# The convolution tail on half tiles: two row pairs of four streams, 64x32 products, and a copy of the odd pairs

## The chip, the cores and the metric

The kernel runs on one core of one Trainium2 chip. A core has a matrix engine (PE, with a separate row PEld for loading its stationary operand), a vector engine (DVE), a scalar engine (ACT), a general engine (POOL) and a queue that issues transfers (SP). PE reads SBUF and writes PSUM, which has eight banks of 512 fp32 columns per partition; DVE and ACT carry results out of PSUM ("eviction"). The metric is the device time of one launch in microseconds. A profile is one further execution, recorded by the hardware.

## The reference, cut to what matters

The input is four images of 16 channels and 512 x 512 pixels, in fp32. Layer 0 (a depthwise convolution, window attention and a perceptron) comes first and is not touched, except for where its result is stored. Then follow:

```
# layer 1: quantise to 8 bits by the largest magnitude, 3x3 convolution, normalise over the whole batch
step = max(abs(x)) / 127;  xq = clip(round(x / step), -127, 127) * step
y = conv3x3(xq, wq);  y = (y - mean(y)) * gamma / sqrt(var(y) + 1e-5) + beta
z = clip(y, 0, 6)
# layer 2: two 3x3 convolutions and a residual
h = relu(conv3x3(z, w1) + b1);  x = conv3x3(h, w2) + b2 + z
# layer 3: a 3x3 convolution and a perceptron 16 -> 128 -> 16 for every pixel
y = conv3x3(x, conv_w);  out = x + w2' relu(w1' y + b1') + b2'
```

Mean and variance of layer 1 need its convolution over the whole batch before any z can be made, so this convolution is done twice: once for the statistics, once for the result.

## The kernel before, in words

`window_attention` is layer 0. It stores its result block by block (`_store_block`, line 88) into `x1`, a buffer in DRAM. `conv_layers` (line 938) is all the rest, called the tail here.

**Tiles.** The image is cut into S = 4 strips of 128 rows. A tile (an index `mm` of M = 64) holds one row pair of each strip of each image: 128 partitions are 4 images x 2 rows x 16 channels, and the free dimension is 4 strips x 512 columns. Row pairs of z, x and the quantised q are offset by one row against those of h and y, so that a 3x3 convolution of an output pair needs two neighbouring input pairs ("sides"), each with three column shifts (dx). Offsetting each layer by one row keeps this alternation.

**A convolution** is therefore 2 sides x 3 shifts x 4 images x 4 strips = 96 products. `_conv_turn` (927) issues four of them: image i's 32 partitions are the contraction, strip j chooses the 32 output partitions, so that all sixteen 32x32 positions of PE's array are used. Layer 1 multiplies in bf16 (integers, exact), the others in fp32; an fp32 product appears in the trace as two matmul instructions. Each shows with its own weight load.

**Turning.** After a convolution, image i's result lies in bank i with the strips along the partitions, so each convolution swaps the two roles. z, h, x, y alternate between the layouts; the residual x is needed in the other layout at the end, and `turned` (1129) copies it with 16 transfers per tile into `xi`.

**The statistics stage** (1037 to 1047): per tile, POOL scales for quantising and ACT rounds (`scaled`, `rounded`), PE convolves into one of two sets of four banks, and DVE takes `bn_stats` of each bank. The loads run eight tiles ahead, in buffers that the main loop uses later. Then `bn_aggr` and a few small operations give scale and shift.

**The main loop** (1210 to 1235) runs 73 steps of 28 slots. In step t, PE convolves y for tile t-4, x for t-3, h for t-1 and z for t; the perceptron's tile is t-6. The table CONVS gives 20 slots of a step to the convolutions. In the other eight, `hidden` (1149) makes the perceptron's 128 hidden values of one row pair by four 32x32 products and one eviction with relu, five of eight by ACT and three by DVE. The four images run two slots apart (LAG), so that products of four row groups, of convolutions and perceptron, are mixed all the time. Convolutions have banks 0 to 3, hidden values banks 4 to 7. At a step's end `outputs` (1165) multiplies the 32 hidden tiles by 128x32 weights, adds the residual and stores the tile.

**Order.** Within the tail the program's order is kept as it is written on PE, DVE, ACT and SP (`manual_schedule`, line 992); waits are set where operands need them. An instruction that waits holds back all behind it on its engine or queue. Evictions of a convolution are `done0` to `done3` (for z, h, x, y), with `clipped` for z; the quantising of tile t+2 is spread over slots 10 to 21.

Of the kernel before, what the change touches and what calls it, by code (L numbers as in the profile page):

```python
# [29 lines left out]
S = 4  # L30
M = H // S // 2
# [19 lines left out]
    ("l3_b1", 1), ("l3_b2", 1), ("head", 2), ("par", 2), ("edge", 2),  # L51
# [36 lines left out]
def _store_block(nc, x1, src, b, r0, cols, queues=None):  # L88

    n = WS // 2  # L90
    s, m = divmod(r0 // 2, M)
    parts = [(1, m, s, 0, n), (0, m + 1, s, 0, n)]
    if m + n == M and s < S - 1:
        parts[1:] = [(0, m + 1, s, 0, n - 1), (0, 0, s + 1, n - 1, 1)]
    for r, mm, ss, at, k in parts:
        part = 32 * b + C * r
        (next(queues) if queues else nc.sync).dma_start(
            x1[mm : mm + k, part : part + C, ss, cols].rearrange("m c x -> c m x"),
            src.rearrange("c (m r) x -> c m r x", r=2)[:, at : at + k, 1 - r],
        )  # L100
# [14 lines left out]
def conv_chain(ctx: ExitStack, tc: tile.TileContext, x, xw, mats, vecs, cqs, cws, hots, out):  # L115
# [6 lines left out]
    x1 = dram.tile([M + 1, P, S, W], F32, name="x1")  # L122
    with tc.tile_pool(name="zeros", bufs=1) as one:
        zero = one.tile([C, W], F32, name="zero")
        nc.vector.memset(zero, 0.0)
        for b in range(B):
            at = 32 * b
            nc.sync.dma_start(x1[0, at : at + C, 0], zero)
            nc.sync.dma_start(x1[M, at + C : at + 2 * C, S - 1], zero)
# [776 lines left out]
def _load_pairs(nc, t, x1, mm):  # L906


    if mm < 0:
        nc.vector.memset(t[:, 0], 0.0)  # L910
        nc.sync.dma_start(t[:, 1:S], x1[M + mm, :, 0 : S - 1])
    elif mm < M:
        nc.sync.dma_start(t, x1[mm])
    else:
        nc.sync.dma_start(t[:, 0 : S - 1], x1[mm - M, :, 1:S])
        if mm == M:
            nc.sync.dma_start(t[:, S - 1], x1[M, :, S - 1])
        else:
            nc.vector.memset(t[:, S - 1], 0.0)


def _turns():

    return [(side, dx, i) for side in range(2) for dx in range(3) for i in range(4)]


def _conv_turn(nc, p, weights, src, side, dx, i):

    for j in range(4):
        nc.tensor.matmul(  # L930
            p[i][_quad(j)], weights[_quad(i), side, dx, :],
            src[side][_quad(i), j, dx : dx + W],
            start=side == 0 and dx == 0, stop=side == 1 and dx == 2,
        )
# [3 lines left out]
def conv_layers(ctx: ExitStack, tc, x1, out, cw, cq, sw, m, v, peak):  # L938
# [5 lines left out]

    nc = tc.nc
    ld = ctx.enter_context(tc.tile_pool(name="l3l", bufs=2))
# [4 lines left out]
    conv_banks, hid_banks = banks[0:4], banks[4:8]  # L963
# [3 lines left out]
    def ring(name, n, dt=F32):  # L967
        tiles = rings[name] = [
            act.tile([P, 4, WP], dt, name=f"{name}{i}") for i in range(n)
        ]  # L970
        return lambda mm: tiles[mm % n]
# [5 lines left out]
    qs = ring("q", 3, BF16)  # L977
    zs, hs, xs, xi, ys = ring("z", 3), ring("h", 2), ring("x", 2), ring("xi", 3), ring("y", 3)
    for name in "qz":
        border(name)  # L980

    edge_b1 = act.tile([P, 2], F32, name="edge_b1")
# [3 lines left out]

    stats = rings["h"][0].rearrange("p s x -> p (s x)")[:, 0 : M * B * 6].rearrange(
        "p (r s) -> p r s", s=6
    )
# [13 lines left out]
    def outside(mm):  # L1003

        return 0 if mm < 0 else S - 1 if mm >= M else None

    loaded = {}

    def load(mm, t=None):
        if t is None:  # L1010
            t = ld.tile([P, S, W], F32, tag="x", name=f"tx{mm}")
        loaded[mm] = t
        _load_pairs(nc, loaded[mm], x1, mm)

    def scaled(mm, at=slice(0, S), engine=nc.vector):
        t = loaded[mm][:, at]
        engine.tensor_scalar(t, t, ix, ROUND, ALU.mult, ALU.add)  # L1017

    def rounded(mm, at=slice(0, S)):
        nc.scalar.activation(  # L1020
            inner(qs(mm))[:, at], loaded[mm][:, at], AF.Identity, bias=unround
        )

    flat = [
        t.rearrange("p s x -> p (s x)")[:, 0 : S * W].rearrange("p (s x) -> p s x", x=W)
        for t in rings["y"] + rings["xi"] + rings["x"]
    ]
    AHEAD = len(flat)  # L1030
    for mm in range(AHEAD):
        load(mm, flat[mm])
    sx, ix = quant_step(nc, act, act, peak, "x")
    for mm in range(2):
        scaled(mm)
        rounded(mm)
    for mm in range(M):
        if mm + 2 <= M:
            scaled(mm + 2, engine=nc.gpsimd)
            rounded(mm + 2)  # L1040
        p = banks[4 * (mm % 2) : 4 * (mm % 2) + 4]
        for turn in _turns():
            _conv_turn(nc, p, cq, (qs(mm), qs(mm + 1)), *turn)
        for b in range(B):
            nc.vector.bn_stats(stats[:, mm * B + b, :], p[b])  # L1045
        if mm + AHEAD <= M:
            load(mm + AHEAD, flat[mm % AHEAD])
    for name in ("x", "xi", "y"):
        border(name)
    for mm in (-2, -1):  # L1050
        load(mm)
        scaled(mm)
        rounded(mm)
    load(0)

# [14 lines left out]
    border("h")  # L1072
# [15 lines left out]
    shift = act.tile([P, 1], F32, name="shift")  # L1088
    ms = mul(mean, scale, "ms")
    nc.vector.tensor_tensor(shift, v("beta"), ms, ALU.subtract)  # L1090


    def done0(mm, b):
        z, p = inner(zs(mm)), conv_banks[b]
        if b % 2:
            nc.vector.tensor_scalar(z[:, b], p, scale, shift, ALU.mult, ALU.add)  # L1096
        else:
            nc.scalar.activation(z[:, b], p, AF.Identity, bias=shift, scale=scale)

    def clipped(mm, b):  # L1100
        z = inner(zs(mm))
        nc.vector.tensor_scalar(z[:, b], z[:, b], ACT_MAX, 0.0, ALU.min, ALU.max)
        if outside(mm) is not None:
            nc.vector.memset(z[_quad(outside(mm)), b], 0.0)

    def done1(mm, s):
        h, p = inner(hs(mm)), conv_banks[s]
        if (s, mm) in ((0, -1), (S - 1, M + 1)):
            nc.vector.memset(h[:, s, :], 0.0)
        elif (s, mm) in ((0, 0), (S - 1, M)):  # L1110
            e = 0 if mm == 0 else 1
            nc.scalar.activation(
                h[:, s, :], p, AF.Relu, bias=edge_b1[:, e : e + 1],
                scale=v("edge")[:, e : e + 1],
            )
        elif s % 2:
            nc.vector.tensor_scalar(h[:, s, :], p, v("l2_b1"), 0.0, ALU.add, ALU.max)  # L1117
        else:
            nc.scalar.activation(h[:, s, :], p, AF.Relu, bias=v("l2_b1"))

    def done2(mm, b):
        x, z = inner(xs(mm)), inner(zs(mm))
        nc.vector.scalar_tensor_tensor(
            x[:, b, :], conv_banks[b], v("l2_b2"), z[:, b, :], ALU.add, ALU.add
        )
        if outside(mm) is not None:
            nc.vector.memset(x[_quad(outside(mm)), b], 0.0)

    def turned(mm):

        if outside(mm) is None:
# [45 lines left out]

    SLOTS, LAG = 28, 2
    CONVS = {}
# [183 lines left out]
```

## Time and profile before

| | us |
|---|---|
| median of 3 runs (6274.52 to 6279.33) | 6274.99 |
| the profiled execution, device time | 6290.58 |
| its span, first to last instruction | 6288.8 |
| PE busy | 6035.0 (96%) |
| ACT busy | 4051.9 (64%) |
| DVE busy | 3220.5 (51%) |
| statistics stage | about 3472 to 3737 |
| main loop, filling | about 3745 to 3924 |
| main loop, steady and end | about 3924 to 6289 |

Busy time of PE counts products whose ends are modelled and that overlap in several positions of the array, so it tells that PE had work, not that it ran at its best. A group of instructions is named by its line, engine and operation, the tiles that it writes and reads, and the shape: 32*32 stands for active rows times columns of the array. The weight loads (PEld) overlap the products. The chain that ended last holds PE for 23% of the span by line 930, 11% by line 1154 and 7% by line 1170.

### The profile page before, as it was taken

How to read it: one execution, taken by the hardware profiler on the slowest of the kernel's cores; microseconds unless marked ns; L12 is line 12 of the kernel's file. 1: busy time of each engine (PE TensorE's matmuls, PEld its weight loads, DVE VectorE, ACT ScalarE, POOL GpSimd, SP SyncE). 2: the span in 40 equal slices, each digit the busy share in tenths (PEclk: the TensorE clock that was granted, in tenths of full speed). 3: DMA queues.
4: the chain of work that ended last, by engine and by line, in shares of the span. 5: the costliest groups of instructions: out<-in, count | busy, mean ns of one | idle time of the engine just before them, and what ended most of it. 6: DMA issues, size and time to landing. Idle time of an engine off the chain costs nothing. (4 is left out here: it accounts for less than half of the span.)

```text
span 6288.8 us, 316830 instructions
## 1 busy us (share of the span) xinstructions
PE 6035.0 (96%) x146976; PEld 3792.6 (60%) x146976; DVE 3220.5 (51%) x4719; ACT 4051.9 (64%) x5602; POOL 150.7 (2%) x127
## 2 busy tenths in 40 slices
PE   8999999999999999999999459999999999999999
PEld 4666666666666666666665336566555555655565
DVE  3444444444444444444444564555555555555555
ACT  4777777777777777777777443555555455555454
POOL 0000000000000000000000530000000000000000
PEclk9999999999999999999999778999999999999999
DMA  3233333232323232323332751222222222222221
GB/s 82 59 76 60 77 60 77 59 78 59 78 59 78 59 78 59 78 58 69 68 61 38 288 201 57 89 86 87 87 89 84 86 89 87 90 86 84 84 82 55
DMA packets 567525, 515.29 MB, mean 82 GB/s; under 512 B 349008, under 2 KB 478352, under 8 KB 545712
## 3 DMA queue, kind: packets, MB, share of 16 engines
q1 hardware_dynamic: 564688, 493.47, 30.0%
q8 instruction: 1154, 18.91, 1.3%
q0 software_dynamic: 1216, 1.05, 0.1%
q14 instruction: 179, 1.47, 0.1%
q10 hardware_dynamic: 288, 0.39, 0.0%
HBM read 225.87 MB, written 134.48 MB: 57 GB/s over the span
## 5 line engine op out<-in xcount | busy, mean ns | idle before, releaser
L1154 PE MATMUL tb<-y,mat 32*32 32x512 f32 x16384 | 1861.5, 597 | 25.0 <-issue 25.0
L1160 ACT ACTIVATE hid<-tb,vec 128x512 f32<-128x512 f32 x1280 | 871.6, 688 | 1143.0 <-PE tb L1154 1082.0
L369 ACT ACTIVATE e<-pair 128x1024 f32<-128x1024 f32 x1024 | 992.4, 1021 | 394.5 <-PE pair L361 394.5
L297 PE MATMUL pair<-x,taps 32*32 32x512 f32 x18432 | 926.5, 604 | 2.6 <-ACT y L308 1.3
L930 PE MATMUL tb<-z,cw 32*32 32x512 f32 x12864 | 902.8, 608 | 5.3 <-issue 5.2
L930 PE MATMUL tb<-h,cw 32*32 32x512 f32 x12672 | 905.8, 604 | 0.0
L1162 DVE TENSOR_SCALAR hid<-tb,vec 128x512 f32<-128x512 f32 x768 | 576.0, 750 | 616.2 <-PE tb L1154 330.0
L930 PE MATMUL tb<-x,cw 32*32 32x512 f32 x12480 | 852.2, 598 | 0.0
L930 PE MATMUL tb<-q,cq 32*32 32x512 bf16 x12672 | 680.8, 447 | 133.7 <-issue 68.8
L417 PE MATMUL bank<-y,fc_e 32*32 32x512 f32 x8192 | 683.1, 603 | 0.9 <-DVE y L409 0.9
L361 PE MATMUL pair<-g,y 32*128 32x128 f32 x16384 | 654.3, 285 | 25.9 <-ACT y L308 24.3
L1154 PEld LDWEIGHTS tb<-y,mat 32*32 32x32 f32 x16384 | 531.1, 103 | 242.7 <-issue 140.1
L361 PEld LDWEIGHTS pair<-g,y 32*128 32x128 f32 x16384 | 544.3, 187 | 214.7 <-issue 109.5
L297 PEld LDWEIGHTS pair<-x,taps 32*32 32x32 f32 x18432 | 602.4, 103 | 97.0 <-issue 17.5
L422 ACT ACTIVATE hid<-bank,f1b 128x512 f32<-128x512 f32 x1024 | 644.8, 685 | 15.5 <-PE bank L417 7.5
L353 DVE COPY yt<-bank 128x512 f32<-128x512 f32 x512 | 347.3, 688 | 550.4 <-PE bank L348 530.8
L930 PEld LDWEIGHTS tb<-h,cw 32*32 32x32 f32 x12672 | 507.3, 104 | 186.8 <-issue 27.0
L380 PE MATMUL bank<-e,yt 128*32 128x128 f32 x16384 | 556.6, 276 | 2.6 <-issue 1.6
L396 DVE TENSOR_TENSOR o<-bank,r 128x512 f32<-128x512 f32 x512 | 354.0, 691 | 372.7 <-ACT r L395 356.8
L385 PE MATMUL bank<-e,hot 128*32 128x512 f32 x4096 | 535.8, 593 | 0.0
L930 PEld LDWEIGHTS <-cq 32*32 32x32 bf16 x12672 | 320.1, 92 | 347.4 <-issue 265.7
L380 PEld LDWEIGHTS bank<-e,yt 128*32 128x32 f32 x16384 | 418.1, 110 | 110.6 <-DVE yt L353 52.8
(163 smaller groups left out, 6770.4 us busy)
## 6 DMA issues: line engine op xcount, KB each, us to landing
x<-in_xw_dram SPq DMA_DIRECT2D x32, 2600.0 KB, 10.8
y<-y SPq DMA_DIRECT2D x2048, 32.0 KB, 2.2
tx<-x SPq DMA_DIRECT2D x64, 1024.0 KB, 5.5
xi<-x SPq DMA_DIRECT2D x1024, 64.0 KB, 2.5
out_dram<-xi SPq DMA_DIRECT2D x64, 1024.0 KB, 4.9
x<-xo SPq DMA_DIRECT2D x1974, 32.0 KB, 1.7
y<-x SPq DMA_DIRECT2D x24, 1024.0 KB, 6.1
xi<-x SPq DMA_DIRECT2D x24, 1024.0 KB, 5.2
```

The lines of the kernel that those rows point to most:

```text
L297: nc.tensor.matmul(bank(u)[quad(vv)], taps[quad(u), tap, :], xts[n // 2][quad(u), vv, dy : dy + WS, at : at + BW], start=tap == 0, stop=ta ...
L361: nc.tensor.matmul(bank(u)[:, P * jj : P * jj + P], y2[quad(u), vv, jl + jj].rearrange("p w t -> p (w t)"), g[quad(u), vv, jl + jj].rearra ...
L369: nc.scalar.activation(e[:, 2 * i : 2 * i + 2].rearrange("p u j t -> p u (j t)"), pairs[i], AF.Exp,)
L380: nc.tensor.matmul(b[quad(u), P * jj : P * jj + P], yt[:, jj, quad(u)], e[:, u, jj, :], start=True, stop=True,)
L385: nc.tensor.matmul(d[quad(u)], own, e[:, u].rearrange("p j t -> p (j t)"), start=True, stop=True,)
L396: nc.vector.tensor_tensor(o[:, vv, jl : jl + 4].rearrange("p j h t -> p (j h t)"), b, r, ALU.mult)
L417: nc.tensor.matmul(b[quad(k)], fc1[quad(vv), quad(k)], y[quad(vv), u, :], start=True, stop=True,)
L422: nc.scalar.activation(hd, b, AF.Gelu, bias=f1b)
L930: nc.tensor.matmul(p[i][_quad(j)], weights[_quad(i), side, dx, :], src[side][_quad(i), j, dx : dx + W], start=side == 0 and dx == 0, stop= ...
L1154: nc.tensor.matmul(p[_quad(c)], w1[_quad(b), 1 - par, 32 * c : 32 * c + 32], inner(ys(mm + par))[_quad(b), s, :], start=True, stop=True,)
L1160: nc.scalar.activation(hd, p, AF.Relu, bias=v("l3_b1"))
L1162: nc.vector.tensor_scalar(hd, p, v("l3_b1"), 0.0, ALU.add, ALU.max)
```

## The change

The tail is written anew on tiles of half the size, and `x1` and the output take a layout to match.

A tile now belongs to one of two pairs of images and one of TP = 64 positions. S is 2: the image has two halves of 256 rows. The 128 partitions are 2 halves x 2 neighbouring row pairs x 2 rows x 16 channels; the free dimension is the 2 images x 512 columns. The four (pair, image) combinations are the streams of a half.

A convolution contracts over 64 partitions, both sides at once, so that three shifts are left: 3 shifts x 2 pairs x 2 images x 2 halves = 24 products of 64 rows and 32 columns (`convolve`). An output pair that straddles two tiles needs its two input pairs in one block of 64 partitions. A second copy of each tile, shifted by one pair, serves these (qo, zo, ho, xo beside qe, ze, he, xe). `shift` makes it by four transfers on SP for each of q, z, h and x: 32 partitions x 2 images x 514 columns each. The result of a convolution has the row pairs and images along the partitions and the halves in the two banks. Weights come in a second copy with the sides exchanged.

The perceptron makes its hidden values in waves: four products of 32 rows and 128 columns, from the four quarters of y into four banks, then four evictions. 16 such products a tile, in two stretches of eight. The output products are 128x32 as before, 16 a tile.

All eight banks are taken in turn by all stages (`take`). In a step, the stages stand one after another: y, eight wave products, x, h, quantising of tile T+2, eight wave products, z, outputs. There are N + 6 = 140 steps, as N = 2 x 67.

The statistics stage uses 64x64 products: both pairs of one image at once, with zero blocks in the weights (`cq2`); 24 products a half tile, bf16. Its loads run 18 half tiles ahead. A load is two transfers of 256 KB. A clip of z is one operation of 1024 columns where there were four of 512; scaling and rounding in the main loop likewise have 1024 columns.

The diff, cut to its core:

```diff
-S = 4
-M = H // S // 2
+S = 2
+TP = H // S // 4
-    x1 = dram.tile([M + 1, P, S, W], F32, name="x1")
+    x1 = dram.tile([H // 2 + 1, 2 * C, B, W], F32, name="x1")
 ...
+def _load_pairs(nc, t, x1, g, tt):
+    for r in range(S):
+        m = r * H // 4 + 2 * tt
+        k = min(2, H // 2 + 1 - m)
 ...
+        nc.sync.dma_start(
+            t[64 * r : 64 * r + 32 * k],
+            x1[m : m + k, :, 2 * g : 2 * g + 2].rearrange("m c f x -> (m c) f x"),
         )
 ...
-    conv_banks, hid_banks = banks[0:4], banks[4:8]
+    turn = itertools.count()
+    def take(n):
+        return [banks[next(turn) % 8] for _ in range(n)]
 ...
+    qe, qo = ring("qe", 3, BF16), ring("qo", 3, BF16)
+    ze, zo, he, ho = ring("ze", 4), ring("zo", 3), ring("he", 2), ring("ho", 2)
+    xe, xo, ye = ring("xe", 5), ring("xo", 3), ring("ye", 3)
 ...
+    for n in range(LAST):
+        if n + 2 < LAST:
+            scaled(n + 2, nc.gpsimd)
+            rounded(n + 2)
+        if n % (TP + 1) < TP:
+            p = take(S)
+            for k in range(2):
+                for dx in range(3):
+                    for f in range(2):
+                        for r in range(S):
+                            nc.tensor.matmul(
+                                p[r][_half(f)], cq2[_half(r), k, dx, :],
+                                qe(n + k)[_half(r), f, dx : dx + W],
+                                start=k == 0 and dx == 0, stop=k == 1 and dx == 2,
+                            )
+            for r in range(S):
+                nc.vector.bn_stats(stats[:, done, :], p[r])
+                done += 1
+        load_flat(n + AHEAD)
 ...
+    def shift(n, e, o):
+        for i in (1, 3):
+            nc.sync.dma_start(o(n)[_quad(i)], e(n)[_quad(i)])
+        if n % K:
+            for i in (0, 2):
+                nc.sync.dma_start(o(n - 1)[_quad(i)], e(n)[_quad(i)])
+    def quantised(n):
+        scaled(n)
+        rounded(n)
+        shift(n, qe, qo)
 ...
+    def convolve(weights, pair):
+        p = take(2)
+        for dx in range(3):
+            for w in range(2):
 ...
+                src, odd = pair[w]
+                for f in range(2):
+                    for r in range(2):
+                        nc.tensor.matmul(
+                            p[r][_quad(2 * f + w)], weights[_half(r), odd, dx, :],
+                            src[_half(r), f, dx : dx + W],
+                            start=dx == 0, stop=dx == 2,
+                        )
+        return p
 ...
+    def stage_z(n):
 ...
+        p, z = convolve(cq, ((qe(n), 0), (qo(n), 1))), inner(ze(n))
+        nc.scalar.activation(z[:, 0], p[0], AF.Identity, bias=shift_by, scale=scale)
+        nc.vector.tensor_scalar(z[:, 1], p[1], scale, shift_by, ALU.mult, ALU.add)
+        nc.vector.tensor_scalar(z, z, ACT_MAX, 0.0, ALU.min, ALU.max)
+        outside(ze(n), t)
+        shift(n, ze, zo)
 ...
+        for q in range(4):
+            w, f = divmod((k + q) % 4, 2)
+            par = w ^ (q % 2)
+            src = ye(n + (w and not q % 2))
             nc.tensor.matmul(
+                p[q], w1[_quad(q), 1 - par, :], inner(src)[_quad(q), f, :],
+                start=True, stop=True,
+            )
+        for q in range(4):
+            w, f = divmod((k + q) % 4, 2)
+            hd = ld.tile([P, W], F32, tag="hid", name=f"hid{n}_{k}_{q}", bufs=24)
+            if next(count) % 8 in (0, 2, 3, 5, 6):
+                nc.scalar.activation(hd, p[q], AF.Relu, bias=v("l3_b1"))
+            else:
+                nc.vector.tensor_scalar(hd, p[q], v("l3_b1"), 0.0, ALU.add, ALU.max)
 ...
+    for T in range(N + 6):
+        if T + 3 < N:
+            load(T + 3, *item(T + 3, -1, TP + 1))
+        stage_y(T - 4)
+        units = wave(T - 6, 0) + wave(T - 6, 1)
+        stage_x(T - 3)
+        stage_h(T - 1)
+        if T + 2 < N:
+            quantised(T + 2)
+        units += wave(T - 6, 2) + wave(T - 6, 3)
+        stage_z(T)
+        outputs(T - 6, units)
```

`stage_h` evicts one bank by ACT and one by DVE, `stage_x` both by DVE with the residual from ze, `stage_y` one each; `stage_h` and `stage_x` end with a `shift`. `outputs` adds the residual in xe and stores the tile. At an image's edge, rows outside are set to zero, and h's edge rows get a scale of zero from a third column of `edge`.

## The prediction

> **What bounds the kernel now.** I read the shares by slice of the span first, then the stretches, then the chain in order of time, then the matrix unit's timeline for one period. In the stretches (first figure the length, then PE, weight loads, DVE, ACT, POOL, with busy time and instructions; last the granted clock, the DMA share, GB/s):
>
> ```profile
> 0.00:3400.00 3400.00, 3332.89 (x74953) 2164.21 (x74956) 1574.37 (x2148) 2628.15 (x3536) 4.67 (x8) 1.00 0.32 67
> ...
> 3472.00:3737.00 265.00, 142.85 (x6144) 98.87 (x6144) 165.32 (x268) 131.77 (x67) 125.84 (x79) 0.74 0.70 266
> 3745.00:3924.00 179.00, 175.54 (x3960) 108.19 (x3964) 82.22 (x159) 61.92 (x93) 0.00 (x0) 0.82 0.21 67
> ...
> 4038.00:6188.00 2150.00, 2123.33 (x56512) 1287.01 (x56496) 1253.55 (x1939) 1091.50 (x1703) 0.00 (x0) 1.00 0.28 85
> ```
>
> The first 3461 us are attention; the change touches only its store addresses. The tail is a statistics stage (3472 to 3737), a filling stage on a lowered clock (3745 to 3924) and a steady loop in which PE never rests, DVE is 58% and ACT 51% busy. The chain in order of time (start, length, group) gives the period and the cost of the output products:
>
> ```profile
> 4038.69 7.06 PE tb L1170 x64
> 4050.07 0.87 PE tb L930 x15
> 4053.93 1.07 PE tb L930 x31
> 4076.15 7.06 PE tb L1170 x64
> ```
>
> From 3923.6 to 6249.4 there are 62 periods: 37.5 us per old tile. Of these, 7.06 are the 64 output products (128x32), 16 groups of four, 441 ns each; 30.4 are the 928 products of 32x32. Those are slower than streaming: 832 fp32 in 52 groups of sixteen and 96 bf16 in 6 should take 52 x 428 + 6 x 220 = 23.6 us, with 428 ns the distance of consecutive passes inside L1170 in the single records. The timeline says where 7 us go (PE only; start, length, line, count):
>
> ```profile
> 4050.35 0.74 PE L1154 MATMUL tb<-y,mat 32*32 32x512 f32 x4
> ...
> 4050.80 0.72 PE L1154 MATMUL tb<-y,mat 32*32 32x512 f32 x4
> ...
> 4051.41 0.66 PE L1154 MATMUL tb<-y,mat 32*32 32x512 f32 x4
> ```
>
> An fp32 product runs as two passes: 0.45 us to the second, but 0.61 to the next product's first. In the records its weight loads come about 190 ns after the streaming of the pass before them has ended, while in L1170 they begin as the pass before starts. 26 fp32 products a tile in each array position x 0.19 is 4.9 us of the 7.
>
> [...]
>
> ```profile
> 2032.76 1.17 PE L361 MATMUL pair<-g,y 32*128 32x128 f32 x32
> 2033.86 1.08 PE L380 MATMUL bank<-e,yt 128*32 128x128 f32 x32
> 2034.76 1.04 PE L385 MATMUL bank<-e,hot 128*32 128x512 f32 x8
> ```
>
> 32x128 with 8 passes of 107 ns (128 columns) takes 1.10 and not 0.86: 0.24; in L1170 7.06 - 16 x 0.428 = 0.21. I take 0.21 a switch. [...] here the statistics stage has 0.74, and its bf16 groups stand 427 ns apart in the records.
>
> **The change, part by part.** The new tile is half the old; P is its period, against 18.75 now.
>
> *PE.* A convolution is 24 products in 8 positions, 3 groups x 2 passes x 0.428 = 2.57 us; y, x and h 7.70; z in bf16 3 x 0.22 = 0.66. [...] I take the loads as hidden. Perceptron: 4 waves x 2 x 0.428 = 3.42 (32x128 loads, 187 ns, fit under 428). Outputs 8 x 0.428 = 3.42. Sum 15.2. Switches: y to waves, waves to x, h to waves, waves to z, z to outputs, outputs to y: 6 x 0.21 = 1.26. Without waits P = 16.5. The weight price (7 us per old tile) goes; six switches per half tile replace two per old tile.
>
> *Evictions, which now sit on the path.* Same number per row pair, but 26 banks are taken in turn of 8, and 8 evictions arrive in 1.7 us. Durations from the groups: ACT hidden 0.69 (0.57 apart in a row), copy 0.58, z 0.77; rounding of 1024 columns 1.15 (0.72 at 512, 2.00 at 2048); DVE hidden 0.75 (0.67 apart), copy 0.69, residual 0.75; scaling of 1024 columns 0.75, clip 0.7 (0.48 and 0.42 at 512). Time 0 is the first product of y. y ends 2.57, waves 0 and 1 run 2.78 to 4.50, x 4.75 to 7.32, h to 9.89; all banks come free in time. h's evictions end at 10.8. Then, in program order, DVE scales tile T+2 (10.75 to 11.5) and ACT rounds it (11.55 to 12.7). Waves 2 and 3 run 10.1 to 11.8, but ACT reaches wave 2's first bank only at 12.6 to 13.3, and z needs this bank: z starts at 13.4 instead of 12.0 and ends at 14.05; queued behind it on PE are the outputs and the next y. The outputs' second bank is wave 2's fourth, freed 14.43: they run 14.5 to 17.96. With the switch **P = 18.2**: 1.7 us of waits. I add 0.2 for issue gaps (the chain shows about 1 us of "issue" in some of the old tiles): 18.4.
>
> *Transfers.* 16 turning copies per old tile go; each half tile gets 16 copies of 128 KB (64 for q), two loads, one store. SP's queue shows what issuing costs:
>
> ```profile
> 4051.59 11.77 SPq L1134 DMA_DIRECT2D xi<-x  x16
> 4063.46 1.43 SPq L913 DMA_DIRECT2D tx<-x  x1
> ```
>
> 0.735 each; 19 x 0.735 = 14 us of 18.4, all in one queue behind waits: x's four copies are issued 9.0 to 11.9, h's (behind them) to 14.9, q's to 17.8, z's (ready 17.0) to 20.7; the store, waiting for the outputs, to 21.4; loads to 22.8; next x at 27. z's land at about 23.2 (2.5 us to landing for 64 KB), which is 5.0 of the next period; h needs them at 7.3. So all hidden, with 2.3 us to spare. Bytes: 2.9 MB in 18.4 us, 157 GB/s; the trace reaches 342 in its best 50 us.
>
> *Filling, draining.* Now 2543.5 (3745.3 to the end) - 64 x 37.5 = 143 us. After: seven iterations before the first wave, each some 8 us (products 2.6 + evicting, clipping and copying about 5): 55; three without waves between the image pairs, 29; stages missing at both ends -33; last store 6: 57. The old fill runs at clock 0.82, with one row group working alone at first; the new order uses all positions.
>
> *Statistics.* 256 evictions as before (0.62 us apart), half the PE instructions, twice the array time (6 groups of four per half tile). On full clock 2 x 1.28 = 2.6 us per old tile, on half 5.1; today's pace is 265 / 64 = 4.1, bank and q waits and missing instructions being its causes in the waits. I take 3.7: -25 us. Bounds: 3.2 (-60, 1 MB at the 342 GB/s above) and 5.4 (+81). Stores two per block instead of up to three, weight placing (six small DVE operations), aggregation over 256 columns as before: nothing, under PE's attention work or within 1 us.
>
> **Sum.** 128 x 18.4 + 57 = 2412 against 2543.5: -131; with -25, -156 on an execution of 6290.6 us (span 6288.8). The median of the runs, 6275, is 15.6 lower; I move it by the same: **6120 us**.
>
> **Rivals.**
> - *Evictions keep pace* (0.13): ACT is only 10.1 and DVE 11.2 us busy of 18; if waits shrink to nothing, P = 16.7: 6275 - (2543.5 - 2195) - 25 = 5900. Against it: ACT's order puts rounding ahead of wave 2.
> - *Statistics on half clock* (0.10): 6120 + 25 + 81 = 6226. For it: 0.74 now; against it: PE would then be busy throughout in all positions, which in the steady loop gives 1.00.
> - *64x32 leaves its weight loads bare as 32x32 does*, (0.16): 9 fp32 groups x 0.19 = 1.7, P = 20.1: 128 x 20.1 + 57 = 2630, +86 - 25: 6336, slower. It decides from P = (2543.5 + 25 - 57) / 128 = 19.6, that is 0.13 us a group. For it: no trace line has 64x32[...].
> - *SP binds, or a switch costs double* (0.09): at 1.05 us an issue, 19 x 1.05 = 20 us; or 6 x 0.42 in place of 1.26 gives P = 19.7: about 6285 to 6330. SP's copies do take 1.2 to 1.8 in single records. Here the change would do nothing.
>
> **How the numbers follow.** 0.52 is for the sum (own range 6050 to 6190), the rest as given. From 5960 (half of the first rival's gain) to 6345 (the third one) holds about 8 in 10. A measurement tells 0.2% (12.5 us) from no change. Faster: 0.52 + 0.13 + 0.10 = 0.75, same 0.05 and slower 0.20, from the last two.
>
> **What would show it.** PE's output group still 3.4 us per 32; passes of 64x32 at 428 throughout (third rival: 428 and 620 in turn); z's products waiting 1 to 1.5 us on a hidden eviction by ACT; the period at 18.4; SP idle 3 to 5 us a period; a fill of 55 us; the statistics stage 240. It is wrong if h or y waits for a copy, if issuing a copy of 4112-byte rows costs more than 1 us, or if a switch costs above 0.4.

## The result and the profile after

The changed kernel takes 6182.1 us (median of four runs, 6168.6 to 6188.2) beside 6277.2 us (6274.5 to 6280.4) for the kernel before: ratio 0.9845, 95% interval 0.9828 to 0.9863, 95 us less. The forecast was 6120, 157 less. Direction and range held, the range by 8 us at its upper end (6190); 62 us of the gain are missing.

The profiled execution is the fastest of the four (span 6166.8 us), 13 us below the median; the profiled one of before lay 13 us above its median. So stages are compared between profiles, and the whole by the medians. These stretches of the changed kernel answer to those of before (length, then PE, weight loads, DVE, ACT and POOL with busy time and instructions; last the granted clock, the DMA share, GB/s):

```profile
0.00:3400.00 3400.00, 3341.93 (x75080) 2167.84 (x75084) 1577.73 (x2152) 2631.69 (x3539) 4.67 (x8) 1.00 0.33 67
3472.00:3737.00 265.00, 192.36 (x3088) 106.29 (x3087) 180.88 (x278) 152.53 (x134) 144.54 (x138) 0.97 0.96 259
3732.00:3831.00 99.00, 70.83 (x920) 28.23 (x904) 34.53 (x57) 26.31 (x36) 0.00 (x0) 0.82 0.63 149
3900.00:6100.00 2200.00, 2039.34 (x27727) 847.02 (x27728) 1268.03 (x1801) 1074.42 (x1672) 0.00 (x0) 1.00 0.64 159
```

Attention is the same. The statistics stage is as long as before, but TensorE's clock went from 0.74 to 0.97 and the DMA share from 0.70 to 0.96 at about the same GB/s: something else has become its limit. The filling stage runs at clock 0.82. In the steady loop the matrix unit has become 93% busy (2039 of 2200; before 2123 of 2150), and the time of weight loads went from 60% of the stretch to 39%.

The chain in order of time gives one period (start, length, work; L1106 is a convolution, L1186 the hidden waves, L1206 the output products):

```profile
4846.57 5.42 PE tb L1106 x96
4851.99 2.00 PE tb L1186 x15
4854.00 0.64 issue
4854.63 0.68 ACT hid L1194
4855.31 0.04 issue
4855.35 0.84 PE tb L1106 x24
4856.19 3.94 PE tb L1206 x32
4860.14 2.74 PE tb L1106 x48
4862.87 2.00 PE tb L1186 x16
4864.88 1.40 PE tb L1106 x17
```

From one group of x and h (96 products) to the next, 4846.57 to 4864.88, are 18.31 us; the median over the run is 18.30, and the forecast was 18.4. x and h together take 5.42 where 12 passes of 0.428 are 5.14. Behind the second waves z stands for 1.36 us, released by a hidden eviction on ACT. The timeline shows why ACT is late (start, length, engine, line, operation; in brackets the idle time before it and what ended it):

```profile
4853.58 1.15 ACT L988 ACTIVATE qe<-tx,unround 128x1024 bf16<-128x1024 f32 x1 [0.86 <-DVE tx L985]
4854.63 2.98 ACT L1194 ACTIVATE hid<-tb,vec 128x512 f32<-128x512 f32 x5
...
4855.35 0.40 PE L1106 MATMUL tb<-qe,cq 64*32 64x512 bf16 x4 [1.29 <-ACT hid L1194]
```

The rounding of the tile of two iterations on (1.15 us, behind 0.86 us in which ACT waits for the scaling on DVE) stands ahead of the five hidden evictions; the first of these frees z's bank. And PE's own timeline of the convolution h:

```profile
4847.82 0.62 PE L1106 MATMUL tb<-he,cw 64*32 64x512 f32 x4
...
4848.25 0.62 PE L1106 MATMUL tb<-he,cw 64*32 64x512 f32 x4
...
4848.68 0.62 PE L1106 MATMUL tb<-he,cw 64*32 64x512 f32 x4
```

Its groups start 0.43 us apart, first pass or second: no weight load of 64x32 is bare, that is, left uncovered by a running product. SyncE's queue over one period:

```profile
4850.95 1.16 SPq L1048 DMA_DIRECT2D xo<-xe  x2
4852.15 1.23 SPq L1051 DMA_DIRECT2D xo<-xe  x2
4853.49 1.17 SPq L1048 DMA_DIRECT2D ho<-he  x2
4854.71 1.22 SPq L1051 DMA_DIRECT2D ho<-he  x2
4856.02 2.09 SPq L1048 DMA_DIRECT2D qo<-qe  x2
```

About 0.6 us a copy; with z's copies, the store and the loads it is busy some 12.4 of 18.3 us.

Between the profiles, then: attention ends some 10 us earlier; the statistics stage, from its first product to the first z product, takes 260 us in place of 264; the main part, from the first z product to the end, 2435.2 us in place of 2543.5, where 2412 was forecast. Main part after: 128 x 18.3 = 2342, and 93 us around it where 57 were forecast.

### The profile page after: what moved, and what is told of

Its sections match the earlier page's. It is cut to its first block, busy times and chain, and to the rows that moved or that the text cites. A ratio compares the mean times of both kernels' runs of the same rounds, so it can differ in the third digit from the quotient of the medians.

```text
span 6166.8 us, 243159 instructions
## 1 busy us (share of the span) xinstructions
PE 5816.3 (94%) x109008; PEld 3219.9 (52%) x109008; DVE 3157.5 (51%) x4425; ACT 3984.1 (65%) x5531; POOL 166.7 (3%) x187
## 3 DMA queue, kind: packets, MB, share of 16 engines
q0 software_dynamic: 1024, 1.05, 0.1%
## 5 line engine op out<-in xcount | busy, mean ns | idle before, releaser
L1194 ACT ACTIVATE hid<-tb,vec 128x512 f32<-128x512 f32 x1280 | 766.0, 689 | 69.5 <-PE tb L1186 69.5
L1196 DVE TENSOR_SCALAR hid<-tb,vec 128x512 f32<-128x512 f32 x768 | 540.9, 745 | 54.3 <-PE tb L1186 45.4
L1186 PE MATMUL tb<-ye,mat 32*128 32x512 f32 x4096 | 546.5, 619 | 0.0
L1206 PE MATMUL tb<-hid,mat 128*32 128x512 f32 x4096 | 511.5, 595 | 0.5 <-ACT hid L1194 0.5
L1170 ACT COPY ye<-tb 128x512 f32<-128x512 f32 x130 | 76.4, 587 | 603.3 <-PE tb L1106 603.3
L307 DVE TENSOR_SCALAR y<-pair,vec 128x512 f32<-128x512 f32 x128 | 90.4, 746 | 705.0 <-PE pair L292 705.0
L343 PEld LDWEIGHTS bank<-mat,y 128*128 128x128 f32 x2048 | 217.2, 141 | 377.8 <-issue 272.0
L1186 PEld LDWEIGHTS tb<-ye,mat 32*128 32x128 f32 x4096 | 246.9, 183 | 302.3 <-issue 263.7
L1106 PE MATMUL tb<-xo,cw 64*32 64x512 f32 x3120 | 370.9, 601 | 12.6 <-DMA xo<-xe 12.6
L1106 PE MATMUL tb<-zo,cw 64*32 64x512 f32 x3120 | 366.4, 591 | 12.6 <-DMA zo<-ze 12.4
```

Source lines behind the costliest of these rows:

```text
L1106: nc.tensor.matmul(p[r][_quad(2 * f + w)], weights[_half(r), odd, dx, :], src[_half(r), f, dx : dx + W], start=dx == 0, stop=dx == 2,)
L1186: nc.tensor.matmul(p[q], w1[_quad(q), 1 - par, :], inner(src)[_quad(q), f, :], start=True, stop=True,)
L1194: nc.scalar.activation(hd, p[q], AF.Relu, bias=v("l3_b1"))
L1196: nc.vector.tensor_scalar(hd, p[q], v("l3_b1"), 0.0, ALU.add, ALU.max)
L1206: nc.tensor.matmul(p[r][_quad(c)], w2[:, par], hd, start=(r, c) not in seen, stop=(r, c) in seen,)
```

## The experiments

### Rounding behind the last waves

```diff
-        if T + 2 < N:
-            quantised(T + 2)
         units += wave(T - 6, 2) + wave(T - 6, 3)
+        if T + 2 < N:
+            quantised(T + 2)
         stage_z(T)
```

> One edit to the changed kernel: the scaling and rounding of the input tile of two iterations on (with its copies) are put behind the last two waves of an iteration instead of ahead of them, still ahead of stage_z. Theory: z's product waits 1.43 us in each iteration because ScalarE works through the rounding (1.15 us) ahead of the hidden evictions that free z's banks; without it that wait is gone, the period falls from 18.3 to about 16.8 us, 128 of them give about 190 us, and the whole run takes 5,980 to 6,010 us. Rival, the odd copies or SyncE set the period: no gain beyond 20 us, 6,160 to 6,190 us. In the filling iterations the order on SyncE stays (copies of q ahead of those of z), so about 13 us each are expected to stay.

Measured: 6006.6 us (6005.3 to 6010.0), ratio to the kernel before 0.9561 [0.9545, 0.9577]: 175.5 us below the changed kernel. The median period is 16.82 us. The chain of this kernel, in order of time:

```profile
4405.71 5.41 PE tb L1106 x96
4411.12 2.07 PE tb L1186 x16
4413.19 0.77 PE tb L1106 x24
4413.97 3.83 PE tb L1206 x32
4417.80 2.74 PE tb L1106 x48
4420.53 2.00 PE tb L1186 x16
```

These six pieces are one period, 16.82 us. z (0.77 us, 24 products) now follows the waves directly; of the 1.36 us nothing is left. The outputs' weaker wait stays for the most part: they take 3.83 us in place of 3.94, where 3.57 is enough in an iteration of this kernel in which they wait for nothing (at 4848.79 us, near the boundary of the image pairs). The place of one ScalarE operation of 1.15 us in program order, with the scaling that it waits for, was worth 1.48 us in every iteration, and 175 us in all are nearly twice what the whole change gained.

### Rounding behind stage_z

```diff
-        if T + 2 < N:
-            quantised(T + 2)
         units += wave(T - 6, 2) + wave(T - 6, 3)
         stage_z(T)
+        if T + 2 < N:
+            quantised(T + 2)
         outputs(T - 6, units)
```

> One edit to the changed kernel: the scaling and rounding of the input tile of two iterations on, with its copies, are put behind stage_z, so that SyncE issues z's copies first. Steady period as with the move to just ahead of stage_z: about 16.8 us. Theory on the filling: an iteration without waves is a chain of z's product, clipping, the issue of z's copies behind q's four on SyncE, their landing and h's product; with z's copies issued first it shortens from 13.2 to 10.5-11 us, which over some 12 such iterations is 25 to 35 us less than with the other move: 5,950 to 5,975 us. Rival, the filling is bound by something else than SyncE's order: the same time as the other move within 10 us.

Measured: 5994.8 us (5988.9 to 5996.8), ratio 0.9542 [0.9526, 0.9558]. The period is 16.82 again. But from the first z product to the first output product it takes 94.1 us beside 97.5 with the other move and 99.4 in the changed kernel, and the interval at the boundary of the image pairs 55.6 beside 59.7 and 58.1. That is 7 us in all between these two profiles, not 25 to 35: this expectation failed. Even the 7 us aren't firm: for the two stretches together this kernel takes 150 us and the one with the other move 157, but two later kernels that copy z first as well take 146 and 155. What holds an iteration without waves is shown by the changed kernel's chain there:

```profile
3762.87 5.11 PE tb L1106 x40
...
3771.47 0.77 DVE he L1146
...
3779.19 2.11 DMA zo<-ze
...
3783.78 3.00 DMA xo<-xe
...
3786.83 7.96 PE tb L1106 x96
```

The same 96 products take 7.96 us here and 5.42 in the loop; each copy adds 2.1 to 3 us of landing (from its issue until its data have arrived), and between evicting and landing lies a queue of copies on SyncE (h's eviction ends at 3772.2, the last of the copies of h, q and z is issued at 3779.2). The reason for the slow products is the clock, in stretches of 8 us (the column before the last two is the granted clock):

```profile
3732.00:3740.00 8.00, 3.31 (x40) 0.84 (x28) 4.40 (x14) 2.02 (x3) 0.00 (x0) 0.50 0.22 49
3748.00:3756.00 8.00, 3.76 (x33) 1.87 (x41) 0.00 (x0) 0.00 (x0) 0.00 (x0) 0.50 0.62 152
3764.00:3772.00 8.00, 7.95 (x115) 3.39 (x102) 2.42 (x4) 0.52 (x1) 0.00 (x0) 0.80 0.69 166
3788.00:3796.00 8.00, 8.00 (x119) 3.03 (x111) 2.50 (x4) 0.59 (x1) 0.00 (x0) 0.80 0.75 180
```

These are means. In the trace the granted clock is either full or half: between 3743 and 3805 us it is half for 3.4 us at a time, once for 10.2, and full for 3.4 to 10.2 us between. Within the 7.96 us above it is half from 3787.7 to 3791.1, and passes stand 0.85 us apart; from then on it is full, and they stand 0.43 apart. Busy time times the missing share of the clock, summed over the stretches from 3732 to 3812, is some 11 us. So the filling has several causes of a few microseconds each: the lowered clock, the queue on SyncE, and the landings.

### q's copies issued twice

```diff
         shift(n, qe, qo)
+        shift(n, qe, qo)
```

> The changed kernel with q's four copies issued twice in each iteration (the second time over the first, the same data): 23 issues on SyncE in place of 19 and 0.5 MB more moved per iteration. Theory: SyncE has 5 to 6 us to spare in each 18.3 us and the DMA engines a third of their time, so the steady part doesn't move (within 15 us over 128 iterations); filling iterations, where z's copies queue behind q's, lengthen by about 2 us each, 20 to 30 us in all: ratio to the kernel before 0.985 to 0.993. Rival, SyncE or the DMA engines set the period: 2.4 us more in each iteration, 300 us in all, ratio 1.03.

Measured: 6225.2 us (6216.0 to 6234.4), ratio 0.9903 [0.9887, 0.992]. The period is 18.30, to 0.01 us that of the changed kernel: four more issues and 0.26 MB of q more to move in every iteration cost the steady loop nothing. (The expectation's 0.5 MB was wrong: q's copies are 64 KB each.) The first output product comes 122.7 us after the first z product in place of 99.4, and the boundary takes 71.5 in place of 58.1: of the 49 us that the main part lost between the profiles, 37 are in iterations without waves, and most of the rest in the four just ahead of the boundary, where stages are already missing. SyncE isn't the limit of the loop, and it is part of the limit of the filling. Additional copies in its queue cost there in full, while taking z's copies out from behind q's returned less; that h's and x's copies and their landings, which come next, are why was not tried.

### Twelve positions in place of sixteen, in the kernel before

```diff
-    for j in range(4):
+    for j in range(n):
...
-        for c in range(4):
+        for c in range(3):
...
-            _conv_turn(nc, conv_banks, weights, (first, second), side, dx, i)
+            _conv_turn(nc, conv_banks, weights, (first, second), side, dx, i, 3)
```

> The kernel before, with the last of the four output column groups left out of the convolutions and of the hidden layer in the main part (the outputs are incomplete): 12 of 16 array positions, 3 of 4 products in each group; evictions, outputs and data movement stay. Theory, the bare weight loads of before (620 ns between the products of one position in place of 428) come from 64 instructions a round [...]: with 48 the gap goes, and the period of a tile falls from 37.5 to 31-33 us though the rounds themselves are as long as before, the run to about 5,900 us. Rival, the geometry (a 32x32 load can't pass a running 32x32 product) makes them: the period stays at 37 to 37.5 us, 6,250 us. Third: TensorE is bound by the number of instructions; then it would be about 30 us.

Measured: 5941.1 us in one run, the median period of a tile 32.1 us in place of 37.5 (as many groups with no bare load would take 23.6 us, as the prediction worked out, and the outputs 7.06, together 30.7). The timeline of PE alone:

```profile
4657.21 0.60 PE L1154 MATMUL tb<-y,mat 32*32 32x512 f32 x3
...
4657.64 0.60 PE L1154 MATMUL tb<-y,mat 32*32 32x512 f32 x3
...
4658.07 0.60 PE L1154 MATMUL tb<-y,mat 32*32 32x512 f32 x3
...
4658.50 0.60 PE L1154 MATMUL tb<-y,mat 32*32 32x512 f32 x3
```

Passes of one position stand 0.43 us apart, where before they stood 0.45 and 0.61 apart in turn. The geometry of the load is the same 32x32, so it isn't that. With a quarter of the products left out, the remaining ones also ran closer. The forecast for 64x32 was made from the number of instructions in a group, loads and products of both passes: 64 in the kernel before, 48 here, 32 with 64x32. That fewer of them leave no load bare was the author's estimate, and it gave the right period here (32.1 us for 31 to 33) and there (18.30 for 18.4). A limit on instructions in a given time is the rival that this run can't exclude: at the old pace, a group in 0.53 us on average, three quarters of a group would take 0.40 us, less than a pass. The trace of the kernel before speaks against it: in its statistics stage sixteen products and their sixteen weight loads begin within 0.06 us (from 3640.43 us on). So the number in a group is the reading that fits all of these, but no run shows how it would act, and between which numbers the gap sets in isn't shown either: only 64, 48 and 32 were run.

### The statistics stage: DRAM layout, row length, number of loads, no loads

Four kernels take the loads apart. In the first, the two images of a half tile lie together in DRAM:

```diff
-    x1 = dram.tile([H // 2 + 1, 2 * C, B, W], F32, name="x1")
+    x1 = dram.tile([2, H // 2 + 1, 2 * C, 2, W], F32, name="x1")
...
-            x1[m : m + k, :, 2 * g : 2 * g + 2].rearrange("m c f x -> (m c) f x"),
+            x1[g, m : m + k].rearrange("m c f x -> (m c) f x"),
```

> The changed kernel with the intermediate image laid out in DRAM so that the two images of a half tile lie together: each load of 256 KB is one contiguous block, its rows still 4,096 bytes long, where before each row is half of an 8,192-byte stretch. Theory, packets of 4,096 bytes are what makes the loads of the statistics stage slow (17.4 bytes per ns and engine against 23.6 with 8,192): nothing changes, the stage stays at 255 to 262 us. Rival, the stride in DRAM makes them slow: the stage falls by 25 to 40 us, to 220 to 235 us.

In the second, a load brings rows of 8,192 bytes for both image pairs, and in the third these loads are cut in two again:

```diff
-            x1[m : m + k, :, 2 * g : 2 * g + 2].rearrange("m c f x -> (m c) f x"),
+            x1[m : m + k, :, 2 * g : 2 * g + n].rearrange("m c f x -> (m c) f x"),
...
-    for n in range(AHEAD):
-        load_flat(n)
+    for t in range(AHEAD):
+        load_flat(t)
```

> The changed kernel with another order of loads in the statistics stage alone: one load brings both image pairs of a row pair (rows of 8,192 bytes, two loads of 512 KB per two half tiles in place of four of 256 KB), and the half tiles of the two pairs take turns. The same bytes, products and statistics. Theory, the rows of 4,096 bytes hold the stage at the DMA engines (17.4 bytes per ns and engine, 1.88 us per half tile of 512 KB): at 23.6 bytes per ns it is 1.39 us, less than the 1.5 us of TensorE and of GpSimd, and the stage falls from about 250-262 us to 215-235; whole run 25 to 40 us shorter, 6,145 to 6,160 us, ratio 0.978 to 0.982. Rival, the stage is at the limit of DRAM or of GpSimd: less than 10 us.

> As the kernel with loads of 8,192-byte rows, but each load cut in two, so that there are four of 256 KB per two half tiles, as many issues on SyncE as in the changed kernel. Theory, the length of the rows counts: as fast in the statistics stage as with two loads, within 5 us. Rival, the number of loads (or their issue on SyncE) counts: the stage is back at 250 to 262 us.

In the fourth, no half tile beyond the eighteenth is loaded:

```diff
     def load_flat(n):
-        if n < LAST:
+        if AHEAD <= n < LAST:
+            loaded[n] = flat[n % AHEAD]
+        elif n < LAST:
```

> The changed kernel with the statistics stage's loads left out beyond the first 18 half tiles; the later half tiles use the 18 again (their values are wrong, GpSimd multiplies by one, all instructions of GpSimd, ScalarE, TensorE and VectorE stay). Theory, the loads hold the stage: it falls from about 255 us to 138 x 1.5-1.6 = 205 to 225 us. Rival, GpSimd, ScalarE or TensorE holds it: 245 us or more.

The stage, from its first statistics operation to its last, took 246 us in the profile of the changed kernel and 255, 261, 263 and 266 in the profiles of four other kernels here that don't touch it, so 246 to 266 is its spread. (By the same measure it took 247 us in the kernel before and 241 in the one with twelve positions, whose statistics stage is the old one.) Contiguous loads: 271 (run 6188.1, ratio 0.9848 [0.9832, 0.9865]). Rows of 8,192 bytes: 252 (run 6191.5, 6172.7 to 6211.9, ratio 0.9833 [0.9805, 0.986]). Rows of 8,192 bytes in twice as many loads: 262 (one run, 6185.8). Without loads: 199 (one run, 6119.0). The loads do hold the stage, by some 47 to 67 us; but neither the stride between the rows in DRAM, nor their length, nor the number of loads is why. The theory of the row length, which the packet times had suggested to me (23.6 bytes per ns and engine for the old rows of 8,192, 17.4 for the new ones of 4,096), fell: in the third of the lines below, rows of 8,192 bytes move no faster. The stretch from 3500 to 3680 us in the changed kernel, with contiguous loads, and with rows of 8,192 bytes:

```profile
3500.00:3680.00 180.00, 141.69 (x2285) 77.81 (x2280) 123.71 (x192) 110.79 (x97) 107.88 (x97) 1.00 1.03 284
```

```profile
3500.00:3680.00 180.00, 128.19 (x2043) 70.70 (x2040) 111.33 (x173) 99.58 (x87) 96.21 (x86) 0.99 1.04 254
```

```profile
3500.00:3680.00 180.00, 133.39 (x2224) 80.27 (x2227) 119.28 (x185) 105.47 (x94) 103.30 (x94) 0.97 1.02 278
```

In all three the DMA engines are busy all the time and move 254 to 284 GB/s. Packets of 8,192 bytes take 475 ns on average in the last, where those of the kernel before took 346.

### Loads over all 128 partitions

What all these kernels with loads share, and the kernel before does not, is that a load reaches at most 64 partitions. So the intermediate image was laid out such that one load fills all 128:

```diff
-    x1 = dram.tile([H // 2 + 1, 2 * C, B, W], F32, name="x1")
+    x1 = dram.tile([H // 8 + 1, P, B, W], F32, name="x1")
...
+    x1 = x1[:, :, 2 * g : 2 * g + 2]
+    if 0 <= tt < TP:
+        nc.sync.dma_start(t, x1[tt])
+        return
```

> The changed kernel with the intermediate image laid out in DRAM as the loads need it, [row group of 128 partitions, 128, image, column], so that a half tile of 512 KB is one load over all 128 partitions, rows of 4,096 bytes, in place of two loads of 256 KB over 64 partitions each; the attention stage's stores of it are cut finer for that (4 to 5 in place of 2 a block). Theory, [...] packets fall back to about 160 ns for 4,096 bytes (26 bytes per ns, as those of 8,192 bytes over 128 partitions took 309 ns before the change), and the statistics stage falls to 200-220 us, near the 199 us without loads; the run to about 6,120-6,145 us if the finer stores cost nothing. Rival, some 280 GB/s is what DRAM gives in this stage: packets stay near 235 ns and the stage at 245-260 us.

Measured: the statistics stage takes 173 us, less than any forecast. A stretch of it:

```profile
4420.00:4540.00 120.00, 119.39 (x2207) 76.63 (x2200) 118.43 (x185) 106.02 (x93) 101.70 (x92) 1.00 1.03 401
```

401 GB/s, so the 254 to 284 of the other kernels weren't what DRAM can give; 4,096 bytes now take a median of 160 ns and a mean of 166 (24.7 bytes per ns and engine) where they took 235. PE is 99% busy at full clock, so the stage is now as long as its products: 173 us over 64 old tiles is 2.7 us each, beside the 2.6 that the prediction had worked out for a full clock. DVE, with 118.4 of 120 us, and the DMA engines have next to nothing to spare either. The stage even beats the kernel without loads, whose clock was 0.93 in its stretch from 3500 to 3660. In the changed kernel some eight loads, for the two halves in turn, are in flight at a time (193 in 180 us, each landing after 7.3 us), and together they still move 284 GB/s. Why the span of 64 partitions goes with the slow packets isn't shown; the new layout also moved the two halves of a tile next to each other in DRAM, which no run tried alone.

The whole run, though, took 7000.6 us, ratio 1.1137 [1.1112, 1.1162]. The finer stores of the attention stage went onto SyncE, and its queue shows what became of that stage:

```profile
1991.85 22.52 SPq L324 DMA_DIRECT2D y<-y  x32
...
2015.11 29.00 SPq L324 DMA_DIRECT2D y<-y  x32
2057.50 52.64 SPq L102 DMA_DIRECT2D x<-xo  x94
```

SyncE is busy for 117 of the 130 us around these lines; a step's stores and the 32 copies of y take turns, and attention ends some 920 us later. The expectation had named this cost and not sized it.

### Both edits, and the stores on two queues

> Both together: rounding behind stage_z, and loads over 128 partitions. If the parts add, 5,995 us less 35 to 50 us: 5,945 to 5,960 us, ratio 0.945 to 0.949. If the finer stores cost the attention stage time, less of it.

Measured: 6818.2 us, ratio 1.0847 [1.0822, 1.0872]; statistics stage 174.5 us, main part 2237.4 us, attention again 920 us longer. The parts do add (182 us below the kernel with the loads alone), but the attention stage swallows them. Its stores were then shared out:

```diff
-                (next(queues) if queues else nc.sync).dma_start(
+                (next(queues) if queues else (nc.sync, nc.gpsimd)[k]).dma_start(
...
-    queues = itertools.cycle((nc.sync, nc.gpsimd))
+    queues = itertools.cycle((nc.sync, nc.gpsimd, nc.scalar))
```

> As the kernel with both edits (rounding behind stage_z, loads over 128 partitions), with every second one of the finer stores of the attention stage issued by GpSimd in place of SyncE, so that SyncE issues as many stores there as in the changed kernel (the last step's stores take turns on SyncE, GpSimd and ScalarE). Theory, the attention stage of the kernels with finer stores was 920 us longer because SyncE, which issues some 32 copies and 64 stores in each 105 us at about 0.55 to 0.9 us, had no time left for another 64: the stage is back at 3,465 to 3,485 us, the statistics stage stays at 173-175 us, the main part at 2,237 us, and the run takes 5,890 to 5,915 us, ratio 0.938 to 0.942. Rival, the 16 KB stores are the price (DMA engines, DRAM): the attention stage stays hundreds of us longer.

Measured: 5922.4 us (5918.9 to 5926.9), ratio 0.9403 [0.9385, 0.942] (the kernel before took 6299.6 us in the same session). This is the fastest version: 260 us below the changed kernel. The first stretch is its statistics stage, the second its steady loop:

```profile
3500.00:3660.00 160.00, 159.98 (x2932) 102.57 (x2928) 157.12 (x246) 141.14 (x124) 136.88 (x124) 0.99 1.02 395
3900.00:5900.00 2000.00, 1987.45 (x27348) 767.66 (x27336) 1260.73 (x1776) 1072.36 (x1652) 0.00 (x0) 1.00 0.69 171
```

PE is busy for over 99% of both, in the first with DVE close behind (157 of 160 us). Attention is back within 20 us of the changed kernel's, so the issues on SyncE were its price and not the smaller stores. The statistics stage begins at 3492.6 us, 8 us beyond what was expected, and the main part takes 2246.8 us, 10 us more; hence 5922 and not 5890 to 5915. Of the main part's 10 us, 8.5 lie in the two stretches without waves (95.2 and 59.4 us, where the same loop took 89.1 and 57.1 in the kernel with both edits). Why they vary so isn't shown.

### Copies without the border columns

```diff
-            nc.sync.dma_start(o(n)[_quad(i)], e(n)[_quad(i)])
+            nc.sync.dma_start(inner(o(n))[_quad(i)], inner(e(n))[_quad(i)])
```

> The changed kernel with the copies of odd pairs moving only the 2 x 512 columns inside the borders (two packets of 2,048 bytes a partition in place of one of 4,112; borders of the copies are set to zero once). Theory, packets of 4,112 bytes are slow for their length (294 ns, 14 bytes per ns, against 85-96 ns for 2,048): the DMA share of the main part falls from 0.64 to about 0.5, copies land 0.1 to 0.2 us earlier, the period stays at 18.3 us, and the filling shortens by 2 to 4 us. Rival, copies from 32 to 32 partitions are slow whatever their packets: packets of 2,048 bytes take about 140 ns, DMA share and landing stay.

Measured: 6184.5 us in one run, period 18.29, DMA share 0.64, landing of z's copies 2.4 us: nothing moved, and the first theory fell. Packets of 2,048 bytes take 133 ns on average here, but those of the output stores, which have the same length, are among them; outside the time of the stores it is 146 ns (14.1 bytes per ns), and the packets of 4,112 took 294 (14.0). The odd length of the rows isn't the price of these copies. The stores span 128 partitions, and in the changed kernel their packets take 96 ns. That the 32 partitions they span are the price of the copies would fit this and the loads' story; it wasn't tried for copies.

## Why the prediction came out as it did

**Period, right.** 18.4 forecast, 18.30 measured. Its terms held one by one: z's wait of about 1.4 us behind the rounding on ScalarE (1.36 in the chain, and removing what it waits for took 1.48 us out of the period), outputs waiting 0.3 (0.37: 3.94 for 3.57), loads of 64x32 hidden. What is left of 18.30 beside these waits and the 15.2 of bare products is 1.4, where six switches, changes from products of one shape to those of another, had 1.26. In the period above, such a change puts the next product off by 0.10 us (outputs to y, 4859.54 to 4860.07, beyond a pass of 0.43) to 0.24 (x and h to waves, 4851.25 to 4851.92); 0.21 for each was the author's estimate from the trace of before.

**Second rival, wrong.** The statistics stage ran at 0.97 of full clock.

**Third rival, wrong.** That the loads of 64x32 would be hidden was the author's estimate. Passes stand 0.43 us apart in groups of 32 instructions in the changed kernel, and in those of 48 in the kernel before with twelve positions: no bare load; so the 32x32 form of a load alone didn't make those of before.

**Fourth rival, wrong for the loop.** SyncE issues a copy in 0.6 us where 0.735 was taken, and four more copies leave the period as it is.

**First rival.** Evictions do keep pace as soon as one operation stands elsewhere: 16.82 us, where the rival had 16.7. The forecast was right to read the order of ScalarE's work as what speaks against it in this change.

**Filling, wrong.** The step "seven iterations before the first wave, each some 8 us: 55" took 86 us, and the three iterations at the boundary 40 in place of 29: 12 to 13 us an iteration. The step took products on a full clock and one queue-free copy; in fact the clock went back and forth between half and full over the first 70 us or so (some 11 us), and in each iteration several copies are issued in one queue and land in 2.1 to 3.4 us (up to 5.7 at the boundary) on the way from one convolution to the next. With 6 us back at the ends it makes the 36 us beyond the 57 forecast. How these 36 us divide beyond the clock's 11, z's place behind q included, is not shown.

**Statistics, wrong.** The step "I take 3.7: -25" came out as nothing that differs from the stage's own spread: 260 us for 264 between the two profiles, and with the other profiles that have the old stage (247 and 241 us) or the new one (246 to 266) rather some 10 us longer than shorter. The full clock came, as that step expected, and the products alone would be 2.7 us per old tile. What it left out is that the new loads span 64 partitions in place of 128; the bound of 342 GB/s, taken from the trace of before, doesn't hold for them (254 to 284). Here the change itself slowed something down: it cost 73 to 93 us against the loads of full width, more than the whole difference from the forecast.

**The sum.** Between the profiles: -108 for the main part where -131 was forecast, -3 for the statistics where -25 was, and some 10 us of attention. The medians say 95 us in all, 27 less than the profiles, since the profiled executions lie 13 us above the one median and 13 below the other. The statistics stage's 246 us in the profile after is the shortest of five, so it has some part in these 27; which stages have the rest isn't shown.

## What to carry to other kernels

When a step is cut into more, smaller steps, look at the transfers first by how many partitions each one spans: loads that span half the partitions cost more here than any row length or stride (254 to 284 GB/s, where those over all 128 partitions reached 401), and no busy share of the kernel before could show it. Then look at what each in-order engine does just ahead of the eviction that frees the next bank; moving one such operation was worth 175 us, nearly twice the change. And when stores are cut finer, count the issues on their queue before anything else: here they made the attention stage some 920 us longer.

## What the runs showed of the hardware

- DMA over 64 partitions a load: 254 to 284 GB/s with engines always busy, rows of 4,096 or 8,192 bytes alike; over 128 partitions 395 to 401 GB/s with the same rows of 4,096 bytes.
- Sixteen array positions with two-pass fp32 products: passes 0.45 and 0.61 us apart in turn; twelve positions of the same shape: 0.43 in the lines shown; eight of 64x32 in the changed kernel: 0.43.
- In the changed kernel's idle-rich filling, after the short pause at the end of the statistics, TensorE's granted clock goes back and forth between half and full until 3805 us, in stretches of 3.4 to 10.2 us (0.50 to 0.95 as the mean of 8 us). While it is half, passes on the chain stand 0.85 us apart in place of 0.43.
- Issuing a copy on SyncE took about 0.6 us in the loop whether it moved 64 or 128 KB; GpSimd issued the attention stage's small stores at about 0.5 us each, while SyncE did the others.
